# Two layers of a graph network on one core: every sixty-fourth tile of gathered rows fetched by SP, one row per transfer

## The chip, the core and the metric

The kernel runs on one core of a Trainium2 chip. A core has five engines with an instruction queue each: TensorE (PE, with its weight loads shown as PEld), VectorE (DVE), ScalarE (ACT), GpSimd (POOL) and SyncE (SP). SP does no arithmetic on data: it issues transfers and waits. The time is that of one execution on the device in microseconds (us); lower is better.

## What is computed

6250 nodes have 160 features each (64 scalars and 32 vectors of three), and 200,000 edges carry messages from a source node to a destination node. Both layers gather the source node's row for each edge, multiply it with the edge's attributes, and sum the messages by destination. Cut to what matters:

```python
# layer 0: s, v = scalars and vectors of x; src, dst = ends of the edges; e0, e1 from edge_attr_4
ss, vv = (s[src], v[src])
m = concatenate([out0(ss, vv, e0, e1), out1(ss, vv, e0, e1)])
m_agg = segment_sum(m, dst, num_segments=n)
x1 = layernorm(x + x + relu(m_agg @ Ws, m_agg @ Wv))

# layer 1: l = linear(x1) * a;  w = relu(edge_attr_10 @ W_fc1) @ W_fc2
y0, y1 = l0[edge_src], l1[edge_src]
m0, m1, m2, m3 = products of w, y0, y1, e0, e1
s = segment_sum(m, edge_dst, num_segments=N)
out = layernorm(x1 + self_interaction(x1) + 0.5 * linear(s))
```

The edges come sorted by destination; the sources are random, so their rows have to be gathered.

## The kernel before

**Tiles and chunks.** The edges are cut into chunks of 512 (`CH`), 391 of them (`NCH`). A chunk is four tiles (`J`) of 128 edges; partition p of a chunk holds edges 4p to 4p+3, and tile j the j-th of each four. `srcs` holds all source numbers on the chip, 128 partitions x 391 chunks x 4. The gathered rows of a chunk are one buffer `G[c]` of 128 x 4 x 160 floats, from a ring of eight buffers (`GRING`, pool `g`).

**The gather.** `gathered` (L241) issues four indirect transfers from POOL for a chunk, one for each tile: each takes 128 row numbers, one of each partition, and fetches 128 rows of 640 bytes from the table in device memory. The table is `in_x` in layer 0 and `ytab` in layer 1; `ytab` is written by layer 0, block by block. The first three chunks of layer 0 go into a buffer of their own, `early`, which later holds edge attributes.

**Order.** The order of the work on each engine is written out by hand (`manual_schedule`), step by step, in the loop at L615. At step t each stage f with a lag handles the chunk at position t − lag of `ORDER` (a list that mixes chunks of the first part of the edges with chunks of the last part). So an engine's queue holds its share of step t, then its share of step t + 1. The stages of layer 0 are `load` at lag 0, `onehot` 1, `add` 3 and `matmuls` 2; those of layer 1 `load` 0, `joined` 4, `onehot` 1, `hidden` 1, `add` 4, `message` 2 and `matmuls` 3, in this order within a step. In words:

- `load` issues the gathers on POOL (L243). In layer 1 it issues on SP the edge attributes `et` for four chunks at a time (L377), into `w_or_et` and `early` in turn. `attributes` (L403) issues on SP the `raw` attributes of up to 32 chunks in four transfers; `turn` has DVE turn them round.
- `onehot` (L416, L420) has DVE build the selection matrices `S` (a ring of three) from `rel` and the attributes.
- `hidden` (L429, L432) has PE and ACT build `h` from `et`; `message` (L442, L445, L450) has PE multiply `h` with `fc2` and DVE multiply the result with `G[c]`.
- `matmuls` (L462) has PE sum by destination, from `G[c]` in layer 0 and from the messages in layer 1; `joined` (L469, ACT) and `add` (L483 to L487, DVE) add the result to the accumulator `acc` at an address that DVE loads into a register (`low`, L475, eight at a time).

**Blocks.** A block is 128 nodes; there are 49. When its last chunk is done (`CLOSE`), the block's own steps are put into the order, some steps later: in layer 0 SP fetches `xt` (L531), PE projects (L506), ACT rectifies and clears (L542, L543), DVE normalises, and at the end `written` sends `ytab` from ACT (L499) and `btab` from SP (L582). In layer 1 SP fetches `base` (L531) and sends `out` (L499).

**Preparation.** At step 8 of layer 0 (`PREPARE`) `prepare` loads the weights: SP issues some 35 small transfers, PE forms five products (L300), DVE puts them in place (L314 to L349).

**SP's queue.** SP issues nearly all transfers other than the gathers, in the order of the steps. A transfer that has to wait (for a buffer, for data to send) holds all those behind it. Each transfer of SP and ACT uses one of eight completion semaphores in turn, and waits for the transfer that used it before.

Of the kernel before, what the change touches and what calls it, by code (L numbers as in the profile page):

```python
# [10 lines left out]
F32 = mybir.dt.float32  # L11
BF16 = mybir.dt.bfloat16
I32 = mybir.dt.int32
AF = mybir.ActivationFunctionType
# [4 lines left out]
P = 128  # L19
N = 6250  # L20
E = 200000
D = 160
M0, M1 = 64, 32
J = 4
CH = P * J
NCH = -(-E // CH)
# [19 lines left out]

FINAL = NCH - 25
AHEAD = 3
FOLD = 104


# [15 lines left out]
def interleaved():  # L67

    units, groups = HALF // 8, list(range(HALF, NCH, 4))
    order = []
    for u in range(units):
        order += range(8 * u, 8 * u + 8)
        while len(groups) > 3 and (17 - (len(groups) - 3) + 1) * units <= (u + 1) * 18:
            order += range(groups[0], min(groups.pop(0) + 4, NCH))
    for g in groups:
        order += range(g, min(g + 4, NCH))
    return order


ORDER = interleaved()
POS = {c: i for i, c in enumerate(ORDER)}
# [33 lines left out]
def gnn_kernel(ctx: ExitStack, tc: tile.TileContext, x, src, dst, ea, sh, avec,  # L117
# [11 lines left out]
    nc = tc.nc  # L129
    weights = (w1t, w2t, w3t, w4t, w5t, ws, wv, wsi0, wsi1, wl10, wl11, w00, w10, w01, w11, wfc1, wfc2)  # L130
    keep = ctx.enter_context(tc.tile_pool(name="keep", bufs=1))
    rel = keep.tile([P, NCH, J], F32, name="rel")
    srcs = keep.tile([P, NCH, J], I32, name="srcs")
    low = keep.tile([1, NWIN + 1], I32, name="low")
    fits = keep.tile([1, 1], I32, name="fits")
    ident = keep.tile([P, P], F32, name="ident")
    ramp = keep.tile([P, P], F32, name="ramp")
    iota = ramp[:, 0:W]
    early = keep.tile([P, AHEAD, J, D], F32, name="early")
    ahead = {}  # L140
    with tc.manual_schedule(), tc.tile_pool(name="ends", bufs=1) as ep, \
# [8 lines left out]

        first = ep.tile([P, AHEAD, J], I32, name="first")
        nc.sync.dma_start(first, src[:, 0:AHEAD, :])
        nc.scalar.dma_start(dsts, dst)
        nc.sync.dma_start(srcs, src)

        for i in range(AHEAD):
            ahead[i] = gathered(nc, early[:, i], first, x, i)
# [22 lines left out]
        late = NCH - HALF  # L180
        folds = [(k, FOLD, slice(FOLD * k, FOLD * k + FOLD)) for k in range(3)]
        folds += [(3 + h, late, slice(HALF + h, NWIN, 2)) for h in range(2)]
        consts = pp.tile([FOLD, 2, 5], F32, name="consts")
        bounds = ep.tile([FOLD, 2, 5], F32, name="bounds")
        ends = ep.tile([FOLD, 2, 5], F32, name="ends")
        nc.vector.memset(bounds[:, 0, :], 1.0)
# [11 lines left out]
        for a, op in enumerate((ALU.max, ALU.min)):  # L198
            nc.vector.tensor_reduce(mm[:, a, :], rel, AX.X, op)
            tp = pp.tile([FOLD, 4, P], F32, name=f"tp{a}")  # L200
            for k in range(4):
                n = FOLD if k < 3 else late
                nc.tensor.transpose(tp[0:n, k, :], mm[:, a, FOLD * k:FOLD * k + n], ident)
# [22 lines left out]
        for rows, wins, chunks in parts:  # L226
            n = chunks.stop - chunks.start
# [5 lines left out]
    go = nc.values_load(fits[0:1, 0:1], min_val=0, max_val=1,  # L233
                        skip_runtime_bounds_check_because="a comparison's result")
    with tc.If(go > 0) as both:
        windowed(tc, x, srcs, rel, low, ident, iota, early, ahead, ea, sh, avec, *weights, out)
    with both.Else():
        general(tc, x, srcs, rel, dst, ea, sh, avec, *weights, out)


def gathered(nc, g, srcs, table, c):  # L241
    for j in range(J):
        nc.gpsimd.indirect_dma_start(out=g[:, j, :], out_offset=None, in_=table,  # L243
                                     in_offset=bass.IndirectOffsetOnAxis(ap=srcs[:, c, j:j + 1], axis=0))
    return g


@with_exitstack
def windowed(ctx: ExitStack, tc: tile.TileContext, x, srcs, rel, low, ident, iota, early, ahead, ea, sh, avec,
             w1t, w2t, w3t, w4t, w5t, ws, wv, wsi0, wsi1, wl10, wl11,  # L250
             w00, w10, w01, w11, wfc1, wfc2, out):

# [3 lines left out]
    nc = tc.nc  # L256
# [94 lines left out]
    def sums(layer, table, gp, hp):  # L351
        with ExitStack() as s:
            wp = s.enter_context(tc.tile_pool(name=f"w{layer}", bufs=2))
            np_ = s.enter_context(tc.tile_pool(name=f"n{layer}", bufs=2))
            if not layer:
                pn = s.enter_context(tc.tile_pool(name="pn", bufs=1, space=PSUM))
                up = s.enter_context(tc.tile_pool(name="up", bufs=1))
            pa = s.enter_context(tc.tile_pool(name=f"pa{layer}", bufs=3 if layer else 4, space=PSUM))
            if layer:
                ph_ = s.enter_context(tc.tile_pool(name="ph", bufs=1, space=PSUM))  # L360
                pp = s.enter_context(tc.tile_pool(name="pp", bufs=2, space=PSUM))
            s.enter_context(tc.manual_schedule())
            G, S, SH, ET, H, M, PA, AT, RAW = {}, {}, {}, {}, {}, {}, {}, {}, {}

            def load(c):
                if layer or c not in ahead:
                    G[c] = gathered(nc, gp.tile([P, J, D], F32, name="g"), srcs, table, c)
                else:
                    G[c] = ahead.pop(c)
                if c % 4 == 0 and layer:  # L370

                    et = w_or_et if POS[c] % 8 >= 4 else early.rearrange("p a j d -> p (a j d)")
                    et = et[:, :2 * CH].rearrange("p (s e) -> p s e", s=2)
                    ET[c // 4] = et
                    for i in range(2):
                        if c + 4 <= NCH:
                            nc.sync.dma_start(et[64 * i:64 * i + 10, :, :],  # L377
                                              ea[:, c * CH:(c + 4) * CH].rearrange("f (s i e) -> f s i e", s=2, i=2)[:, :, i, :])
                        else:
                            for k in range(c + i, NCH, 2):  # L380
                                nc.sync.dma_start(et[64 * i:64 * i + 10, (k - c) // 2, :], ea[:, k * CH:(k + 1) * CH])
                for first, n in GROUPS:
                    if fetched[first] == POS[c]:
                        attributes(first, n)
# [12 lines left out]
            def attributes(first, n):  # L397

                raw = RAW[first] = hp.tile([P, 512], F32, name="raw")
                if n < 32:  # L400
                    nc.vector.memset(raw, 0.0)
                for q in range(4):
                    nc.sync.dma_start(raw[32 * q:32 * q + n, :],  # L403
                                      sh[first:first + n, 32 * q:32 * q + 32, :].rearrange("c p f -> c (p f)"))
# [115 lines left out]
            def normed(name, b):  # L520
                r = rows(b)
                rs = np_.tile([P, 1], F32, name="rs")
                nc.vector.reciprocal(rs[:r], T.pop(("sd", b))[:r])  # L523
                o = T[name, b] = T.pop(("z", b))
                nc.vector.tensor_scalar(o[:r], o[:r], T.pop(("mv", b))[:r, 0:1], rs[:r],  # L525
                                        op0=ALU.subtract, op1=ALU.mult)
# [77 lines left out]
                sent_rows(nc.sync, b, out[b * P:b * P + rows(b), :], T.pop(("o", b)))  # L604

            if layer:
                stages = [(load, 0), (joined, 4), (onehot, 1), (hidden, 1), (add, 4), (message, 2), (matmuls, 3)]
                parts = [(fetch_base, 3, 2), (project_last, 5, 4), (residual_last, 6, 5), (deviation, 7, 5),
                         (sent, 8, 6)]
            else:  # L610
                stages = [(load, 0), (onehot, 1), (add, 3), (matmuls, 2)]
                parts = [(fetch, 4, 1), (project, 6, 3), (rectify, 6, 4), (residual, 8, 4), (deviation, 9, 4),
                         (lambda b: normed("x1", b), 10, 5), (turned, 11, 5), (kept, 12, 5), (linear, 13, 7),
                         (written, 14, 7)]
# [15 lines left out]
    with tc.tile_pool(name="g", bufs=GRING) as gp, tc.tile_pool(name="sh", bufs=1) as hp:  # L630
        sums(0, x, gp, hp)
        sums(1, ytab, gp, hp)
# [388 lines left out]
```

## Time and profile before

| | us |
|---|---|
| median of three runs | 3960.12 (3959.2 to 3963.18) |
| the profiled execution | 3964.59 |
| its span, first to last instruction | 3962.8 |
| mean granted TensorE clock | 0.78 (0.57 between 100 and 1950 us, 0.99 between 1990 and 3930) |
| gathers from `in_x` in the ring: 1552 | busy 1468.9, mean 0.946 each, idle before them 472.8 |
| gathers from `ytab`: 1564 | busy 1479.2, mean 0.946 each, idle before them 497.7 |

The two layers are about equally long: layer 0 ends near 1960 us, layer 1 begins at 1984. In a list of waits each line has the engine and line that waited, what ended the wait, the total in us, how often, and the longest. "issue" is time in which an engine waited for nothing that the profile shows. In a timeline a line has the start, the duration, engine, line, operation, what is written and read, how many instructions are merged into the line, and in brackets the idle time before it and what ended it. SPq, ACTq and DVEq are the engines' queues: issues of transfers, register loads, waits. An SP line's duration is that of the issue, not of the transfer.

### The profile page before, as it was taken

How to read it: one execution, taken by the hardware profiler on the slowest of the kernel's cores; microseconds unless marked ns; L12 is line 12 of the kernel's file. 1: busy time of each engine (PE TensorE's matmuls, PEld its weight loads, DVE VectorE, ACT ScalarE, POOL GpSimd, SP SyncE). 2: the span in 40 equal slices, each digit the busy share in tenths (PEclk: the TensorE clock that was granted, in tenths of full speed). 3: DMA queues.
4: the chain of work that ended last, by engine and by line, in shares of the span. 5: the costliest groups of instructions: out<-in, count | busy, mean ns of one | idle time of the engine just before them, and what ended most of it. 6: DMA issues, size and time to landing. Idle time of an engine off the chain costs nothing. (4 is left out here: it accounts for less than half of the span.)

```text
span 3962.8 us, 42550 instructions
## 1 busy us (share of the span) xinstructions
PE 3250.1 (82%) x12754; PEld 2152.7 (54%) x12755; DVE 2032.2 (51%) x6485; ACT 478.4 (12%) x1217; POOL 2960.1 (75%) x3133
## 2 busy tenths in 40 slices
PE   4777777777777777777788898998999999999998
PEld 3444444444444445455555566665666666666665
DVE  4223222233333333344456666666666677777776
ACT  2000000000000000001111111111111111111111
POOL 7777777777777777777677777777777777777775
PEclk7555555565565656566699999999999999999999
DMA  3222222223232323233222222222333333232332
GB/s 86 74 66 66 71 74 69 74 71 79 71 77 74 76 72 78 75 79 81 71 72 73 71 76 73 75 74 74 75 80 76 78 76 77 74 81 75 80 77 66
DMA packets 198440, 295.63 MB, mean 75 GB/s; under 512 B 59462, under 2 KB 140860, under 8 KB 198202
## 3 DMA queue, kind: packets, MB, share of 16 engines
q0 software_dynamic: 150144, 256.45, 26.3%
q1 hardware_dynamic: 40870, 31.56, 2.7%
q10 hardware_dynamic: 7188, 4.80, 0.4%
q8 instruction: 107, 1.75, 0.2%
q14 instruction: 131, 1.07, 0.1%
HBM read 280.57 MB, written 12.00 MB: 74 GB/s over the span
## 5 line engine op out<-in xcount | busy, mean ns | idle before, releaser
L243 POOL DMA_INDIRECT g<-ytab,srcs x1564 | 1479.2, 946 | 497.7 <-issue 394.5
L243 POOL DMA_INDIRECT g<-in_x,srcs x1552 | 1468.9, 946 | 472.8 <-issue 396.3
L462 PE MATMUL ab<-g,S 128*128 128x160 f32 (+1 forms) x3736 | 1177.5, 494 | 502.4 <-DMA g<-in_x,srcs 380.6
L462 PEld LDWEIGHTS ab<-g,S 128*128 128x128 f32 (+1 forms) x3736 | 724.5, 287 | 964.9 <-DMA g<-in_x,srcs 669.5
L462 PE MATMUL ab<-m,S 128*128 128x320 f32 (+1 forms) x3760 | 958.3, 446 | 6.8 <-DVE acc L487 6.3
L442 PE MATMUL pw<-fc,h 100*128 100x192 f32 x3128 | 663.5, 343 | 158.2 <-DVE m L450 73.8
L442 PEld LDWEIGHTS pw<-fc,h 100*128 100x128 f32 x3128 | 503.8, 191 | 426.1 <-issue 301.5
L462 PEld LDWEIGHTS ab<-m,S 128*128 128x128 f32 (+1 forms) x3760 | 612.5, 193 | 220.7 <-issue 40.7
L485 DVE STREAM_TRANSPOSE ab<-ab 128x160 f32<-128x160 f32 x470 | 170.5, 363 | 946.1 <-PE ab L462 944.0
L445 DVE TENSOR_TENSOR m<-pw,g 128x256 f32<-128x256 f32 x782 | 330.3, 422 | 520.8 <-DMA g<-ytab,srcs 439.1
L450 DVE TENSOR_TENSOR m<-g,pw 128x192 f32<-128x192 f32 x1564 | 475.9, 346 | 0.0
L420 DVE TENSOR_TENSOR S<-bank,sh 128x384 f32<-128x384 f32 (+2 forms) x782 | 431.5, 552 | 65.9 <-PE ab L462 15.8
L487 DVE TENSOR_TENSOR acc<-acc,ab 128x120 f32 (+2 forms) x940 | 261.4, 278 | 212.8 <-ACT acc L543 140.2
L469 ACT ACTIVATE ab<-ab 32x160 f32<-32x160 f32 x470 | 121.2, 265 | 1350.8 <-PE ab L462 1151.9
L432 ACT ACTIVATE h<-ph 100x512 f32<-100x512 f32 x391 | 228.5, 585 | 207.4 <-PE ph L429 203.6
L416 DVE TENSOR_TENSOR bank<-ramp,rel 128x96 f32<-128x96 f32 (+2 forms) x782 | 199.4, 255 | 21.3 <-PE bank L593 21.0
L483 DVE STREAM_TRANSPOSE ab<-ab 128x160 f32<-128x160 f32 x470 | 167.4, 356 | 13.1 <-issue 8.5
L506 PE MATMUL ph<-w_or_et,acc 128*128 128x160 f32 (+1 forms) x490 | 138.1, 466 | 1.7 <-DVE acc L487 1.3
L506 PEld LDWEIGHTS ph<-w_or_et,acc 128*128 128x128 f32 (+1 forms) x490 | 129.2, 328 | 11.9 <-issue 8.8
L542 ACT ACTIVATE rl<-ph 128x160 f32<-128x160 f32 (+1 forms) x49 | 14.9, 303 | 931.2 <-PE ph L506 930.6
L429 PE MATMUL ph<-early,fc 10*100 10x512 f32 x392 | 112.5, 637 | 2.4 <-DMA early<-in_ea 2.4
L429 PE MATMUL ph<-w_or_et,fc 10*100 10x512 f32 x390 | 109.8, 632 | 1.8 <-DMA w_or_et<-in_ea 1.8
(94 smaller groups left out, 820.0 us busy)
## 6 DMA issues: line engine op xcount, KB each, us to landing
g<-ytab,srcs POOLq DMA_INDIRECT x1564
g<-in_x,srcs POOLq DMA_INDIRECT x1552
raw<-in_sh SPq DMA_DIRECT2D x88, 64.0 KB
early<-in_ea SPq DMA_DIRECT2D x98, 40.0 KB
xt<-in_x SPq DMA_DIRECT2D x48, 80.0 KB
ytab<-y ACTq DMA_DIRECT2D x48, 80.0 KB
btab<-base SPq DMA_DIRECT2D x48, 80.0 KB
w_or_et<-in_ea SPq DMA_DIRECT2D x96, 40.0 KB
```

What stands on the lines that cost most here:

```text
L243: nc.gpsimd.indirect_dma_start(out=g[:, j, :], out_offset=None, in_=table, in_offset=bass.IndirectOffsetOnAxis(ap=srcs[:, c, j:j + 1], axi ...
L416: nc.vector.tensor_tensor(oh[:, :, :w], iota[:, None, :w].to_broadcast([P, J, w]), rel[:, c, :, None].to_broadcast([P, J, w]), op=ALU.is_e ...
L420: nc.vector.tensor_tensor(S[c][:, :, :, :w], oh[:, :, None, :w].to_broadcast([P, J, 4, w]), attr[:, :, :, None].to_broadcast([P, J, 4, w]) ...
L429: nc.tensor.matmul(ph[:, i, :], fc1[g:g + 10, :], ET[c // 4][g:g + 10, c % 4 // 2, :], start=True, stop=True)
L432: nc.scalar.activation(H[c], H["p"][:, c % 2, :].rearrange("f (p j) -> f j p", j=J), AF.Relu, scale=FC_SCALE)
L442: nc.tensor.matmul(pw[:, j, :], h[:, q + j, :], fc2, start=True, stop=True)
L445: nc.vector.tensor_tensor(mq[:, :, :, 0:64], pw[:, :, 0:128].rearrange("p j (a u) -> p j a u", a=2), y[:, :, None, 0:64].to_broadcast([P, ...
L450: nc.vector.tensor_tensor(mq[:, :, a, 64:160].rearrange("p j (d u) -> p j d u", d=3), y1, pw[:, :, None, w:w + 32].to_broadcast([P, 2, 3, ...
L462: nc.tensor.matmul(ab[:, :n], one[h * i:h * i + h, j, :, :], t[h * i:h * i + h, j, :], start=(j == 0), stop=(j == J - 1), skip_group_check ...
L485: nc.vector.transpose(tr, blocks[:, 0])
L487: nc.vector.tensor_tensor(v, v, tr[:, :, :width(c)], op=ALU.add)
L506: nc.tensor.matmul(po[:r], lhs, weights[:, g, :], start=(g == 0), stop=(g == 4))
```

## The change

At positions 15, 31, 47, ... 383 of both layers, 24 in each, POOL issues three gathers for the chunk, and not four. The rows of the chunk's last tile come by SP. They are spread over the sixteen steps up to the chunk's own `load`: at each step SP loads eight row numbers of the tile into eight registers (one instruction), and then issues eight transfers of one row of 640 bytes, from an address made of the register, to one partition of a buffer `row` (two of these). The program has one instruction of register arithmetic ahead of each such transfer. The numbers of a tile are fetched as one line of 128 from `in_src` to a single partition (`num`), half a period ahead. At the step after the chunk's `load`, ACT copies the buffer `row` into the last tile of `G[c]`; the copy is the first thing in ACT's queue of that step, and waits for the rows and for the chunk's three gathers. In SP's queue the rows of a step stand ahead of everything else of the step.

All else is as before: the rings, the lags, the arithmetic. SP's program grows from 681 transfers to 6873 (with the general path, which isn't taken), with 6144 instructions of register arithmetic and 768 loads of eight registers; POOL's has 48 gathers fewer, ACT's 48 copies more.

```diff
+EVERY = 16
+ROWS = P // EVERY
...
-def gathered(nc, g, srcs, table, c):
-    for j in range(J):
+def gathered(nc, g, srcs, table, c, tiles=J):
+    for j in range(tiles):
         nc.gpsimd.indirect_dma_start(out=g[:, j, :], out_offset=None, in_=table,
                                      in_offset=bass.IndirectOffsetOnAxis(ap=srcs[:, c, j:j + 1], axis=0))
...
+            rp = s.enter_context(tc.tile_pool(name=f"r{layer}", bufs=2))
...
+            helpers = {EVERY - 1: (nc.sync, mybir.EngineType.SP)}
+            helped = {ORDER[i] for i in range(EVERY // 2, NCH) if i % EVERY in helpers}
+
+            def numbers(c):
+                NUM[c] = rp.tile([1, P], I32, name=f"num{POS[c] % EVERY}")
+                nc.sync.dma_start(NUM[c], src[:, c, J - 1:J].rearrange("p a -> a p"))
+
+            def fetch_rows(c):
+                i = POS[c]
+                for place, (queue, engine) in helpers.items():
+
+                    k = (i - place - 1) % EVERY
+                    due = i - k + EVERY - 1
+                    if due >= NCH or ORDER[due] not in helped:
+                        continue
+                    d = ORDER[due]
+                    if d not in NUM:
+                        numbers(d)
+                    if d not in ROW:
+                        ROW[d] = rp.tile([P, D], F32, name=f"row{place}")
+                    if k == EVERY // 2 and due + EVERY < NCH:
+                        numbers(ORDER[due + EVERY])
+                    a = k * ROWS
+                    _, at = nc.values_load_multi_w_load_instructions(
+                        NUM[d][0:1, a:a + ROWS], engines=[engine], min_val=0, max_val=N - 1,
+                        skip_runtime_bounds_check_because="node numbers")
+                    for n in range(ROWS):
+                        queue.dma_start(ROW[d][a + n:a + n + 1, :], table[ds(at[n], 1), :])
+
+            def place_rows(c):
+                if c in helped:
+                    del NUM[c]
+                    nc.scalar.activation(G[c][:, J - 1, :], ROW.pop(c), AF.Copy)
+
             def load(c):
                 if layer or c not in ahead:
-                    G[c] = gathered(nc, gp.tile([P, J, D], F32, name="g"), srcs, table, c)
+                    G[c] = gathered(nc, gp.tile([P, J, D], F32, name="g"), srcs, table, c, J - (c in helped))
...
-                stages = [(load, 0), (joined, 4), (onehot, 1), (hidden, 1), (add, 4), (message, 2), (matmuls, 3)]
+                stages = [(fetch_rows, 0), (load, 0), (place_rows, 1), (joined, 4), (onehot, 1), (hidden, 1), (add, 4), (message, 2), (matmuls, 3)]
...
-                stages = [(load, 0), (onehot, 1), (add, 3), (matmuls, 2)]
+                stages = [(fetch_rows, 0), (load, 0), (place_rows, 1), (onehot, 1), (add, 3), (matmuls, 2)]
```

In the changed program `fetch_rows` issues the numbers at L375, loads the registers at L393 and issues the rows at L397; the copy of `place_rows` is L402, and the gathers are L246.

More of the change, by code (lines that the diff above doesn't have):

```diff
@@ L235, in gnn_kernel @@
     with tc.If(go > 0) as both:
-        windowed(tc, x, srcs, rel, low, ident, iota, early, ahead, ea, sh, avec, *weights, out)
+        windowed(tc, x, srcs, src, rel, low, ident, iota, early, ahead, ea, sh, avec, *weights, out)
     with both.Else():
         general(tc, x, srcs, rel, dst, ea, sh, avec, *weights, out)
-def gathered(nc, g, srcs, table, c):
-    for j in range(J):
+def gathered(nc, g, srcs, table, c, tiles=J):
+    for j in range(tiles):
         nc.gpsimd.indirect_dma_start(out=g[:, j, :], out_offset=None, in_=table,
@@ L248, in windowed @@
 @with_exitstack
-def windowed(ctx: ExitStack, tc: tile.TileContext, x, srcs, rel, low, ident, iota, early, ahead, ea, sh, avec,
+def windowed(ctx: ExitStack, tc: tile.TileContext, x, srcs, src, rel, low, ident, iota, early, ahead, ea, sh, avec,
              w1t, w2t, w3t, w4t, w5t, ws, wv, wsi0, wsi1, wl10, wl11,
@@ L362, in sums @@
             s.enter_context(tc.manual_schedule())
-            G, S, SH, ET, H, M, PA, AT, RAW = {}, {}, {}, {}, {}, {}, {}, {}, {}
+            G, S, SH, ET, H, M, PA, AT, RAW, NUM, ROW = ({} for _ in range(11))
+            helpers = {EVERY - 1: (nc.sync, mybir.EngineType.SP)}
[27 more added lines that the diff above has]
+                    nc.scalar.activation(G[c][:, J - 1, :], ROW.pop(c), AF.Copy)
             def load(c):
                 if layer or c not in ahead:
-                    G[c] = gathered(nc, gp.tile([P, J, D], F32, name="g"), srcs, table, c)
+                    G[c] = gathered(nc, gp.tile([P, J, D], F32, name="g"), srcs, table, c, J - (c in helped))
                 else:
```

## The prediction

> **What bounds the kernel now.** I read the page's busy times first, then the waits of POOL, then POOL's timeline, then who waits for the gathers, and last the rows of SP.
>
> ```profile
> span 3962.8 us, 42550 instructions
> PE 3250.1 (82%) x12754; PEld 2152.7 (54%) x12755; DVE 2032.2 (51%) x6485; ACT 478.4 (12%) x1217; POOL 2960.1 (75%) x3133
> ...
> POOL 7777777777777777777677777777777777777775
> ```
>
> PE is the busiest, yet POOL is the engine whose digit never changes. Its waits (total us, times, longest) say why:
>
> ```profile
> POOL g L243 <- issue: 790.8, 2596, 0.3
> POOL g L243 <- PE ab L462: 60.9, 200, 0.3
> ...
> POOL g L243 <- DMA ytab<-y: 21.6, 1, 21.6
> ```
>
> Every idle stretch is 0.3 us, whatever is named as its end, except one of 21.6 us between the layers. So POOL's 25% of idle time is the fixed gap between two gathers, and not waiting. Its timeline at the layer boundary shows the beat (start, duration, and the idle time before in brackets):
>
> ```profile
> 1959.14 0.95 POOL L243 DMA_INDIRECT g<-in_x,srcs  x1 [0.30 <-issue]
> 1960.39 0.95 POOL L243 DMA_INDIRECT g<-in_x,srcs  x1 [0.30 <-issue]
> 1961.64 0.94 POOL L243 DMA_INDIRECT g<-in_x,srcs  x1 [0.30 <-issue]
> 1984.20 0.94 POOL L243 DMA_INDIRECT g<-ytab,srcs  x1 [21.62 <-DMA ytab<-y]
> ```
>
> The first layer's 1552 ring gathers start at 21.21 us and the last at 1961.64: 1940.43 / 1551 = 1.251 us each. The second layer's 1564 run from 1984.20 to 3938.61: 1954.41 / 1563 = 1.250. A chunk of four gathers takes 5.00 us, and 391 chunks twice are almost the whole span. The consumers wait for it:
>
> ```profile
> PEld ab L462 <- DMA g<-in_x,srcs: 669.5, 894, 2.2
> DVE m L445 <- DMA g<-ytab,srcs: 439.1, 400, 2.5
> ```
>
> In layer 1 the slack of the next engine is small: between 1990 and 3930 us PE is busy 1778.41 us of 1940, that is 4.58 us of a 5.00 us chunk.
>
> **What the change takes away.** At positions 15, 31, ... 383 (24 in each layer) POOL issues three gathers for the chunk, not four: 48 × 1.25 = 60.0 us off the beat that sets the span. A period of 16 chunks takes 63 × 1.25 = 78.8 us, or 4.92 us a chunk. PE's 4.58 still fits, and DVE's wait of 439.1 / 391 = 1.1 us a chunk is more than the 0.08 asked of it.
>
> **What it adds on SP.** At every one of the 384 steps of a layer up to position 383 SP loads eight node numbers into registers, then issues eight transfers of one row, each with an instruction of register arithmetic ahead of it. The trace has no transfer with an address from a register, so I bound a row from the nearest lines (min/median/max ns):
>
> ```profile
> L582 SPq DMA_DIRECT2D btab<-base x49: 246/327/352, 401.9 to 1981.1; - x49
> L377 SPq DMA_DIRECT2D early<-in_ea x98: 282/300/1455, 30.7 to 3889.7; - x98
> L475 DVEq TENSOR_LOAD <-low x118: 593/596/1149, 28.0 to 3937.2; - x118
> L487 DVEq FUSED_REGOPS  x940: 69/69/69, 29.2 to 3949.9; - x188
> 68.39 0.42 SPq L340 DMA_DIRECT2D wc<-in_w  x1
> 68.86 0.89 SPq L342 DMA_DIRECT2D wc<-in_w  x2
> 69.79 0.42 SPq L343 DMA_DIRECT2D wc<-in_w  x1
> ```
>
> Issue: 0.246 us is the shortest (the last block, 106 rows), 0.282 the shortest of 20 runs of 2 KB, 0.42 that of a back-to-back burst of 32 rows, whose pitch (68.39 to 69.79, three transfers) is 0.465, hence 0.045 between instructions. I take 0.30, near the low end, since one row is the smallest transfer, with 0.05 for the unseen address. Register arithmetic: DVE's 0.069. A row is 0.069 + 0.045 + 0.30 + 0.045 = 0.46 us; with the ends 0.246 and 0.42 it is 0.405 and 0.58. The load of eight registers is 0.596 + 0.045 = 0.64, from DVE's row. A step: 8 × 0.46 + 0.64 = 4.32 (3.88 to 5.28).
>
> SP's older work by step: layer 0 per 16 chunks two blocks (0.40 + 0.33 + gaps, 1.6 us), two raw transfers (0.9), one of node numbers (0.5): 3.0 / 16 = 0.19. Layer 1 has eight et transfers of 0.35 as well, with base and out of two blocks: 6.2 / 16 = 0.39. So SP needs 4.51 us a chunk in layer 0 and 4.71 in layer 1 against POOL's 4.92. It keeps up as long as a row costs below (4.92 − 0.64 − 0.19) / 8 = 0.51 us, or 0.49 in layer 1. That is the whole question.
>
> Completion: in the built program each SP transfer waits for the one eight before it. In the burst above the 14 transfers of wc keep 0.465 without a stall, so each landed within 8 × 0.465 = 3.7 us; eight rows take 3.68. No added wait, if rows land no slower.
>
> The Trainium skill speaks against the change: "DMA: Bandwidth & Descriptors", section "Rules for kernel authors", tells to coalesce many small transfers, and its section "Anatomy of one DMA — SWDGE (gpsimd) path" gives about 2.0 us fixed for one. By it, as an estimate, 128 rows one after the other would take 256 us. The burst's row, 0.465 apart, shows that they overlap, and decides. The same page's section "Issuing engines are not separate DMA queues" holds that issuing elsewhere only saves sequencer time, usually small; here POOL's beat is such time, and it is the span.
>
> **What is queued behind SP's new work.** The first raw transfers (18.90 us) move behind two number loads, their landing, a register load and eight rows: 0.93 + 1.0 + 0.64 + 3.68, to 25.1. The weights of `prepare` stand behind nine steps, 8 × 4.32 after raw: they begin near 62 and, at their present durations (5.4 and 11.4 us), end near 78.6 in place of 73.0. DVE waits for wc till 74.50 now, and PE goes on with chunk 8 at 76.72, so that chunk is done at 82.3 + 1.5 = 83.8. POOL needs its ring slot for chunk 16 at 81.2 + 3.75 = 85.0: covered by 1 us. Row 15's last part then lands near 78.6 + 7 × 4.32 + 2 = 111, chunk 15 is done near 113, and POOL needs its slot at 85 + 35 = 120. Covered by 7 us; later SP gains (4.92 − 4.51) × 16 = 6.6 us a period. At 0.51 us a row both covers are gone.
>
> Later SP is held at a block's store (L582, L499) until the computation reaches the same step, about three chunks behind POOL. A row issued then is needed after about two more chunks, 10 us, against 4.3 to issue and 2 to land: covered. At the layer boundary SP begins layer 1's rows with POOL at 1984 and ends the first tile after 16 × 4.71 = 75 us, POOL's chunk 15 after 79.
>
> **On ACT**: 48 copies of 128x160, about 0.3 us each by L542's 303 ns, ACT busy 12%. The copy stands at step 16k, ahead of `joined` and `hidden`, and waits for the chunk's three gathers too. That holds layer 1's chain some 4 us once in 16 chunks, made good at 4.92 − 4.58 = 0.34 a chunk; the eight slots cover 39 us. Only after position 383 is there no time left to make it good: +1 us at the end.
>
> **Sum.** Against the profiled run's own 3964.6 us (span 3962.8 and 1.8 around it): −60.0 + 1 = 3905.6. The median of the three runs, 3960.1, is 4.5 below the profiled one, so the forecast is 3901, with 3897 to 3915 for this case (nothing lost, or 14 us lost at the start).
>
> **Rivals.** *SP becomes the bound* (slower). Place: L397 in the new program. For it: the burst's 0.42 is as much a row as 0.30 is, and it gives 0.58 a row. Against it: the shorter issues of the smaller transfers. It decides from 0.50 us a row; beyond it each 0.01 costs 768 × 8 × 0.01 = 61 us. At 0.52: about 3900 + 122 = 4020. At 0.58: 384 × (5.47 + 5.67) = 4278, plus the 120 us of start, boundary and ends: about 4400.
>
> *Half of it*: layer 1 stays at 5.00 us, since SP needs just 0.2 us less than POOL there, or PE and the waiting copy eat the slack: 3960 − 30 + 1 = 3931. For it: PE's 92% there. Against it: DVE's 1.1 us of waiting.
>
> *Nothing*: rows land so late that the ring fills each period and gives back what was won: 3960. For it: only SP's narrow margin; the eight slots speak against it.
>
> **Chances.** Forecast case 0.60, half 0.06, no change 0.04, SP the bound 0.30. A change under 0.2% can't be told from none here, so faster 0.66, same 0.04, slower 0.30. Within the slow case half lies beyond 0.535 us a row, 4110 us, so the range goes from 3896 to 4100 and leaves some 0.15 above and 0.04 below.
>
> **What would show it.** Right: SP's row issues at L397 pitched 0.40 to 0.50 us; POOL's timeline still at 1.25 us with no waits above 0.3 but at the boundary; 3068 gathers. Wrong: a pitch above 0.51, POOL waiting for ACT or PE once a period, or ACT's L402 waiting long for the row transfers while SP has no wait of its own. If POOL's beat between gathers itself lengthens, the sum's first term is wrong.

## The result, and the profile after

| | kernel before | kernel after |
|---|---|---|
| median, us | 3960.12 (3958.48 to 3963.18, 5 runs) | 3992.21 (3985.14 to 4001.66, 5 runs) |
| the profiled execution | 3964.59 | 3998.08 |
| its span | 3962.8 | 3996.3 |

The ratio is 1.0079, with a 95% interval of 1.0068 to 1.009: slower by 0.8%, where 1.5% faster was forecast. The time lies in the stated range (3896 to 4100), on the wrong side of the kernel before.

First the page of the kernel after, the lines that answer to those shown of before:

```profile
span 3996.3 us, 62132 instructions
...
PE 2984.6 (75%) x12754; PEld 2126.7 (53%) x12755; DVE 2004.4 (50%) x6485; ACT 486.5 (12%) x1265; POOL 2917.6 (73%) x3085
...
POOL 7777777777777777777477777777777777667663
```

POOL's digit is now 4 in one slice in the middle, and falls towards the end. The list of waits of the same kernel (total us, times, longest) says what is new:

```profile
POOL g L246 <- issue: 822.2, 2687, 3.0
ACT g L402 <- DMA row<-in_x: 722.0, 23, 71.9
...
DVE z L587 <- DMA xt<-in_x: 290.3, 27, 21.6
...
PE ph L468 <- DMA early<-in_ea: 75.9, 26, 8.8
...
POOL g L246 <- DVE m L489: 40.8, 65, 4.8
...
POOL g L246 <- DMA row<-ytab: 37.5, 1, 37.5
```

Three kinds of transfer that are SP's come late: `xt` (a block's rows of layer 0; before, the list had no such wait), `et` (into `early` and `w_or_et`; before, PE waited 2.4 and 1.8 us for it in all, now 75.9 and 53.9), and the new rows. The ring's gathers on POOL now wait up to 4.8 us for DVE, where before none of their waits but the one at the boundary passed 0.3. POOL's timeline at that boundary:

```profile
1934.12 0.94 POOL L246 DMA_INDIRECT g<-in_x,srcs  x1 [0.30 <-issue]
1972.55 0.94 POOL L246 DMA_INDIRECT g<-ytab,srcs  x1 [37.49 <-DMA row<-ytab]
```

From the first and last gathers in such timelines the span falls into four parts. The last column is the kernel with the two edits found below; the shortfall is the kernel after minus that one (each figure is rounded by itself).

| us of the profiled span | before | after | both edits | shortfall of after |
|---|---|---|---|---|
| to the end of layer 0's last gather | 1962.6 | 1935.1 | 1934.3 | 0.7 |
| wait at the boundary | 21.6 | 37.5 | 15.2 | 22.3 |
| layer 1, first to last gather | 1955.4 | 1975.0 | 1927.0 | 48.0 |
| from there to the end | 23.2 | 48.8 | 17.7 | 31.1 |
| sum | 3962.8 | 3996.3 | 3894.2 | 102.1 |

Layer 0 gains POOL 27.5 us of the 30 forecast. All that is lost is lost at the boundary, in the second half of layer 1 and after the last gather.

**The price of a row was not the cause.** The rows of SP by line (ns: min/median/max), of the kernel after:

```profile
L397 SPq FUSED_REGOPS  x6144: 37/37/51, 21.8 to 3935.9; - x199
L397 SPq MOVE row<-in_x x3072: 29/29/38, 21.9 to 1926.5; - x192
L397 SPq DMA_DIRECT2D row<-in_x x3072: 224/228/322, 22.0 to 1926.6; - x192
```

```profile
L393 SPq TENSOR_LOAD <-num x768: 550/782/983, 21.2 to 3932.2; - x192
```

A row is one instruction of register arithmetic, a move and the issue, with short gaps: 0.411 us from one to the next (median), below the 0.46 that was taken and the 0.51 at which SP would have become the bound. A step by these is 8 × 0.411 + 0.78 = 4.07, and a tenth of all steps, from the start of one to the start of the next, are done in 4.13 us or less. Yet SP took (1926.6 − 22.0) / 384 = 4.96 us a step in layer 0 and (3936.0 − 1971.7) / 384 = 5.12 in layer 1, where POOL's own pace is 4.92. The rest is SP's older transfers and waiting.

**Layer 0: SP waits for ACT, several steps ahead.** The largest but one of SP's own waits, of the same kernel:

```profile
SPq L397 <- DMA ytab<-y: 163.4, 31, 18.8
```

31 times a row transfer waits for `ytab`, 163.4 us in all. A row of `in_x` has no need of `ytab`; what they share is the eight completion semaphores. One of these waits is 16.6 us long and ends at 502.02. ACT's timeline there, with the transfer that ends it:

```profile
499.88 0.39 ACT L616 ACTIVATE y<-pl,a_sb 128x160 f32<-128x160 f32 x1 [11.46 <-PE pl L610]
500.31 0.34 ACTq L538 DMA_DIRECT2D ytab<-y  x1
```

The order in the program as built shows how the two are tied. These are SP's transfers with the number of the semaphore that each waits for and takes over, read from the list of its instructions, with the steps counted by the register loads (the transfers in the trace have the same turns):

```
step 97  row  semaphores 3 4 - 6 7 0 1 2 3      5 is left out: ACT's ytab has it
step 98  row  semaphores 4 5 6 7 0 1 2 3        the second row waits for that ytab
...
step 101 row  semaphores 5 6 7 0 1 2 3 4
step 101 btab semaphore 5                       btab of the same block
```

The block's `ytab` belongs to step 101: the `btab` that the code issues right after it is SP's last transfer of step 101. But its turn among the eight came in SP's step 97. The semaphores were not dealt in the order of the steps; ACT's transfer was put 4 steps early here, and 7 for the next block (taken in step 103, `btab` in step 110). So SP, at step 98, waits until the computation has done step 101. It can't be ahead; it is pinned behind. By the timelines SP loads the numbers of step 104 at 527.4 us, 15.8 us after DVE built that step's selection matrix, and those of step 184 at 941.7, 36.5 us after. (With the two edits of the next section these are 510.2 and 902.7 us, 1.2 and 0.1 before DVE's.) Everything else that SP sends stands in that queue, `xt` too, fetched only four steps ahead of its use. The ring of eight hides it from POOL, so layer 0 loses nothing until its end, where the last blocks' `ytab` come late: 37.5 us.

**Layer 1: a loop through SP.** A stretch of the chain of work that ended last (start, us, what), of the kernel after:

```profile
3462.29 0.97 SPq L393
...
3466.39 0.23 SPq L397
...
3466.71 1.90 DMA early<-in_ea
...
3468.75 1.60 PE ph L468 x4
3470.36 2.86 PE pw L481 x8
3473.22 3.94 PE ab L501 x8
...
3484.43 0.36 DVE z L564
3484.79 0.22 DVE bank L455
3485.01 0.19 SPq L538
...
3485.24 0.93 SPq L393
```

Read it as a circle. SP loads eight numbers and issues eight rows (4.4 us); only then `et` (1.90 us), which PE needs one step later (`hidden`, L468); PE and DVE work; DVE finishes a block; SP's store of that block (L538) has waited for it; and behind the store stand the next rows and the next `et`. One turn here is 22.95 us for four steps, 5.7 us a step against POOL's 4.92. PE waited for `et` before 3300 us too, 76 of the 130 us in all, and POOL kept its beat; why the circle closes only there isn't shown. Once it is closed it is the pace: from 3312 us on POOL took 79.0 to 90.5 us for 63 gathers (16 chunks), and not 78.8.

### The profile page after: what moved, and what is told of

It is laid out like the page before. It is cut to its first block, busy times and chain, and to the rows that moved or that the text cites. A ratio compares the mean times of both kernels' runs of the same rounds, so it can differ in the third digit from the quotient of the medians.

```text
span 3996.3 us, 62132 instructions
## 1 busy us (share of the span) xinstructions
PE 2984.6 (75%) x12754; PEld 2126.7 (53%) x12755; DVE 2004.4 (50%) x6485; ACT 486.5 (12%) x1265; POOL 2917.6 (73%) x3085
## 4 chain that ended last, share of the span: by engine, by line
PE 34%; SPq 23%; issue 16%; POOL 11%; DMA 10%; DVE 5%; ACT 1%; DVEq 0%; ACTq 0%; POOLq 0%
PE ab L501 17%; SPq L397 16%; POOL g L246 11%; PE pw L481 9%; SPq L393 5%; PE ph L468 4%; DMA g<-in_x,srcs 4%; DMA g<-ytab,srcs 2%; DVE m L489 1%; PE bank L632 1%; DMA early<-in_ea 1%; DMA w_or_et<-in_ea 1%; PE ph L545 1%; PE pl L610 1%; DVE m L484 1%
## 5 line engine op out<-in xcount | busy, mean ns | idle before, releaser
L246 POOL DMA_INDIRECT g<-ytab,srcs x1540 | 1458.1, 947 | 554.4 <-issue 405.3
L246 POOL DMA_INDIRECT g<-in_x,srcs x1528 | 1447.1, 947 | 466.4 <-issue 416.9
L501 PE MATMUL ab<-g,S 128*128 128x160 f32 (+1 forms) x3736 | 904.2, 432 | 738.3 <-ACT g L402 315.9
L501 PEld LDWEIGHTS ab<-g,S 128*128 128x128 f32 (+1 forms) x3736 | 649.0, 264 | 996.1 <-DMA g<-in_x,srcs 340.0
L501 PE MATMUL ab<-m,S 128*128 128x320 f32 (+1 forms) x3760 | 986.7, 459 | 2.3 <-DVE acc L526 2.1
L501 PEld LDWEIGHTS ab<-m,S 128*128 128x128 f32 (+1 forms) x3760 | 635.9, 202 | 227.5 <-issue 61.9
L481 PEld LDWEIGHTS pw<-fc,h 100*128 100x128 f32 x3128 | 551.5, 203 | 243.5 <-issue 153.1
L524 DVE STREAM_TRANSPOSE ab<-ab 128x160 f32<-128x160 f32 x470 | 168.7, 359 | 564.5 <-PE ab L501 560.4
L468 PE MATMUL ph<-early,fc 10*100 10x512 f32 x392 | 131.8, 680 | 76.2 <-DMA early<-in_ea 75.9
L468 PE MATMUL ph<-w_or_et,fc 10*100 10x512 f32 x390 | 126.6, 658 | 54.4 <-DMA w_or_et<-in_ea 53.9
L545 PE MATMUL ph<-w_or_et,acc 128*128 128x160 f32 (+1 forms) x490 | 113.7, 401 | 40.6 <-DVE acc L526 40.1
L545 PEld LDWEIGHTS ph<-w_or_et,acc 128*128 128x128 f32 (+1 forms) x490 | 103.5, 270 | 51.4 <-issue 42.5
```

The lines of the kernel that those rows point to most:

```text
L468: nc.tensor.matmul(ph[:, i, :], fc1[g:g + 10, :], ET[c // 4][g:g + 10, c % 4 // 2, :], start=True, stop=True)
L481: nc.tensor.matmul(pw[:, j, :], h[:, q + j, :], fc2, start=True, stop=True)
L501: nc.tensor.matmul(ab[:, :n], one[h * i:h * i + h, j, :, :], t[h * i:h * i + h, j, :], start=(j == 0), stop=(j == J - 1), skip_group_check ...
L545: nc.tensor.matmul(po[:r], lhs, weights[:, g, :], start=(g == 0), stop=(g == 4))
```

## The experiments

Two edits undo one of these each, and leave rows, register loads and copies as they are. The first, in `written`:

```diff
-                sent_rows(nc.scalar, b, ytab[b * P:b * P + r, :], y)
+                sent_rows(nc.sync, b, ytab[b * P:b * P + r, :], y)
```

The second takes the `et` part out of `load` into a stage of its own, three steps earlier:

```diff
+            def edges(c):
+                if c % 4 == 0:
...
-                stages = [(fetch_rows, 0), (load, 0), (place_rows, 1), (joined, 4), (onehot, 1), (hidden, 1), (add, 4), (message, 2), (matmuls, 3)]
+                stages = [(edges, -3), (fetch_rows, 0), (load, 0), (place_rows, 1), (joined, 4), (onehot, 1), (hidden, 1), (add, 4), (message, 2), (matmuls, 3)]
...
+            if layer:
+                for i in range(3):
+                    edges(ORDER[i])
```

The first edit changes two things at once, the engine that sends `ytab` and the place of its turn among the semaphores.

A third kernel gives the rows four steps more of lead, to test the rival that rows late at ACT's copy are all there is to it (at the price of two tiles, 46 and not 48):

```diff
-            helped = {ORDER[i] for i in range(EVERY // 2, NCH) if i % EVERY in helpers}
+            helped = {ORDER[i] for i in range(EVERY, NCH) if i % EVERY in helpers}
...
-                i = POS[c]
+                i = POS[c] + 4
                 for place, (queue, engine) in helpers.items():
```

**The first four runs.** ytab by SP:

> The changed kernel, with one edit: in layer 0 ytab is sent by SP, right before btab, and no longer by ACT. Theory (completion semaphores): SP and ACT share eight of them, dealt in turn when the program is built; there the ytab transfer of a block stands up to 7 steps before SP's rows of the same step, so a row at SP's step 97 waits for ytab of step 101, and SP runs 14 to 37 us behind DVE in layer 0. With ytab in SP's own order this wait (163 us in 31 waits at L397) goes, SP runs level with DVE or ahead, DVE's wait for xt (290 us) goes, and the wait of POOL at the boundary falls from 37.5 to about 22 us: 3992 - 16 = 3976; layer 1 as it is. Rival (SP's work): SP is late because rows take too long to issue; 49 more transfers of 0.35 us make it later: 3992 to 4000, xt as late as before. Rival (rows late at ACT's copy alone): as the first, no change, 3992.

et earlier:

> The changed kernel, with one edit in layer 1: the edge attributes et of a group of four chunks are issued by SP three steps before the step in which they stand now, where they come behind the eight rows of their step and are needed one step later. Theory (a loop through SP): in the second half of layer 1 et lands late, PE's hidden layer waits, DVE then ends the block late, SP's out store waits for DVE, and the next rows and et stand behind that store. With et three steps (12 to 15 us) earlier the loop opens: PE's waits for et (130 us in all) go, the beat of POOL holds, layer 1's gathers take 1925 and not 1975 us, and the tail after the last gather is about 24 and not 49 us: 3992 - 50 - 25 = 3918; up to 3945 if the rows, still one step ahead of their use, hold ACT. Rival (SP's work): SP issues as much as now, so it stays as late: 3992. Rival (rows late at ACT's copy): 3985 to 3992.

Both:

> The changed kernel with both edits, ytab sent by SP in layer 0 and et three steps earlier in layer 1. Theory (semaphores and loop): the gains add, 3918 - 16 = 3902, close to 60 us below the kernel before; up to 3930 if rows still hold ACT. Rival (SP's work): 3992 or more. Rival (rows late at ACT's copy): 3985 to 3992.

Rows with more lead:

> The changed kernel with one edit: the sixteen steps over which a tile's rows are issued end four steps earlier (five steps of lead at ACT's copy, not one); the tile at position 15 is gathered by POOL in both layers, so 46 gathers fewer, not 48 (+2.5 us). SP's work, ytab and et stay. Theory (semaphores and loop): ACT's copy no longer waits for rows in layer 1, but et still lands late and SP is still held by ytab: 3980 to 4000. Rival (rows late at ACT's copy are what holds the chain): the copies' waits and the lateness both go: 3905 to 3930. Rival (SP's work): 3992, rows later again by as much as SP falls behind.

None came out as any theory had it. On this chip the kernel before itself took 4829.63 us, and the four took 5843.61, 5884.34, 5883.23 and 5714.75. SP was slow in a way that the first profile doesn't have, so the kernel after was run beside the edits once more:

> The changed kernel itself, beside the next three on one chip. The four runs so far were on a chip where the kernel before took 4830 us, not 3960, and where SP, in stretches, started its instructions only 0.70 or 1.40 us apart (some 1600 such intervals; none in the changed kernel's first profile); they say nothing on the two theories. On a chip where the kernel before takes 3960: 3992. On one where it takes 4830: about 5880, like the four kernels that differ little from it.

> The edit of e1_ytab_sp again (ytab sent by SP, in SP's own order). On a chip where the kernel before takes 3960: theory (completion semaphores) 3976, POOL's wait at the boundary 22 and not 37 us, DVE's wait for xt gone; rival (SP's work) 3992 to 4000 with xt as late as before.

> The edit of e2_et_early again (et three steps earlier in layer 1). On a chip where the kernel before takes 3960: theory (loop through SP) 3918, up to 3945 if the rows hold ACT; layer 1's gathers take 1925 and not 1975 us. Rival (SP's work) 3992.

> The edits of e3_both again (both). On a chip where the kernel before takes 3960: theory 3902, up to 3930 if the rows hold ACT; rival (SP's work) 3992 or more.

That was another such chip: before 4866.12, after 5948.73, ytab by SP 5945.53, et earlier 5977.19, both 5982.9. SP's row transfers, of the kernel after on that chip:

```profile
L397 SPq DMA_DIRECT2D row<-in_x x3072: 1/228/1406, 22.6 to 3001.2; - x192
```

The median is that of the first chip, 228 ns, but single ones last 1.4 us: in stretches SP starts an instruction every 0.70 or 1.40 us, whatever it is. The mean pitch of rows within a step is 0.79 us (0.45 on the first chip), and a step takes 7.59 us on average (5.10). SP waited 313 of the 5914 us of the profiled span there, against 492 of 3996 on the first chip. That speaks for SP's issuing as the bound there, but it isn't shown; PE and POOL, too, were held for hundreds of us by causes that this profile doesn't name. The edits did not help: on the second such chip they moved the time by −3 to +34 us. More lead for the rows (5714.75, ratio 1.1828 against 1.2107 for ytab by SP on that chip) helped some. Why the kernel before takes 22% more there too isn't known, since no profile of it was had on such a chip. The run meant for that met a chip like the first:

> The kernel before itself, for its profile on the chip at hand. On the two chips of the first eight runs it took 4830 and 4866 us, not 3960, and the changed kernel 5949. If the chip is like the first one: 3960, POOL's beat 1.25 us throughout. If it is like those two, two theories: (a) every gather takes longer or is further apart, a beat near 1.53 us throughout; (b) the beat is 1.25 us wherever POOL can go on, and there are holes in which engines wait for nothing that the profile shows (PE's weight loads on 'issue', as for 1015 us in the changed kernel there), because instructions reach the engines late. In (b) a program with 20,000 instructions on SP in place of 900 is hit the hardest on SP.

It took 3960.11 us, which leaves both theories on the slow chips untried. Eight more runs of the same edits followed. Three fell on a slow chip at once:

> The edit of e1_ytab_sp (ytab sent by SP, in SP's own order), meant for a chip where the kernel before takes 3960, as it did in the last run. Theory (completion semaphores): 3976, POOL's wait at the boundary 22 and not 37 us, SP's 163 us of waiting for ytab and DVE's 290 us of waiting for xt gone. Rival (SP's work): 3992 to 4000 with xt as late as before.

> The edit of e2_et_early (et three steps earlier in layer 1), for a chip where the kernel before takes 3960. Theory (loop through SP): 3918, up to 3945 if the rows hold ACT; layer 1's gathers take 1925 and not 1975 us. Rival (SP's work): 3992.

> The edits of e3_both (both), for a chip where the kernel before takes 3960. Theory: 3902, up to 3930 if the rows hold ACT; rival (SP's work): 3992 or more.

5950.63, 5985.04 and 5995.69 us, before 4872.0. And two later, meant to divide the gain between the edits:

> The edit of layer 0 alone (ytab sent by SP), on a chip where the kernel before takes 3960. If the two edits act each in its own layer: POOL's wait at the boundary is 15 us as with both edits, layer 0's gathers end at 1934, and layer 1 is as in the changed kernel (gathers 1975 us, tail 49 us), so the span is 1949 + 1975 + 49 = 3973 and the time 3975. If the lateness of layer 1 is carried over from layer 0: near 3895 to 3920. On a chip like the slow ones 5950.

> The edit of layer 1 alone (et three steps earlier), on a chip where the kernel before takes 3960. If the two edits act each in its own layer: layer 0 and the boundary as in the changed kernel (layer 1 begins at 1972.6), and layer 1 as with both edits (gathers 1927 us, tail 18 us): 1972.6 + 1927 + 17.7 = 3917, time 3919. If layer 1 needs both: above 3950. On a chip like the slow ones 5980.

5852.89 and 5886.97 us, before 4823.59: no more is learnt from these five than from the first. What follows is from the three that met chips on which the kernel before takes 3960 to 3962.

**Both edits.**

> The two edits of e3_both in one kernel: ytab sent by SP (layer 0), et three steps earlier (layer 1). On a chip where the kernel before takes 3960: theory (semaphores in layer 0, a loop through SP in layer 1) 3902, up to 3930 if the rows hold ACT. In layer 0 SP's waits for ytab and DVE's for xt go and POOL waits 22 and not 37 us at the boundary; in layer 1 the gathers take 1925 and not 1975 us and the tail is 24 and not 49 us. Rival (SP's work): 3992 or more, layer 0's xt as late as before, layer 1's gathers 1975 us. On a chip like the slow ones: 5950 to 6000, and the question stays open.

3895.26 us (3893.95 to 3896.72), ratio 0.9835 (0.9819 to 0.9851): faster than the kernel before by 1.6% and than the kernel after by 97 us. The theory's 3902 is met within 7 us; the boundary and the end came out 7 and 6 us better than it had them. SP's issue work, the rival, is out: SP issues the same rows at the same 228 ns, and 50 transfers more. Its list of waits for POOL, which answers to the first one:

```profile
POOL g L246 <- issue: 771.7, 2532, 0.3
...
POOL g L246 <- DMA row<-ytab: 15.2, 1, 15.2
```

No wait of the ring's gathers but the boundary's passes 0.3 us, apart from one for PE of 1.1. DVE's wait for `xt` and PE's for `et` are gone from the list. SP still waits, for the data that it has to send:

```profile
SPq L540 <- ACT y L618: 151.6, 34, 11.4
SPq L540 <- DVE bank L457: 93.6, 36, 11.2
```

These waits don't show in POOL's beat. SP is level with DVE: it loads the numbers of step 336 at 3598.3 us, DVE builds that step's matrix at 3598.4. In layer 1 the rows of every tile are issued 5.6 to 18.7 us before the chunk's own gathers are done.

**Each alone.** Layer 0's edit:

> The edit of layer 0 alone (ytab sent by SP), on a chip where the kernel before takes 3960. Each edit acting in its own layer: boundary wait 15 us, layer 1 as in the changed kernel (gathers 1975 us, tail 49 us): 3975. If layer 1's lateness is carried over from layer 0: 3895 to 3920. On a chip like the slow ones 5950.

3973.23 us (3966.2 to 3979.41), ratio 1.0034 (1.0022 to 1.0045). Its waits:

```profile
PE ph L468 <- DMA early<-in_ea: 74.6, 27, 8.0
...
POOL g L246 <- DMA row<-ytab: 15.6, 1, 15.6
```

The boundary is 15.6 us, SP's waits at the rows for `ytab` are gone from its list, though SP now has `ytab` itself to send, and layer 1 is as slow as in the kernel after (1972.0 us of gathers, 48.9 after them): each edit acts in its own layer. Layer 1's edit:

> The edit of layer 1 alone (et three steps earlier), on a chip where the kernel before takes 3960. Each edit acting in its own layer: layer 1 begins at 1973 as in the changed kernel and takes 1927 us of gathers and 18 us of tail as with both: 3919. If layer 1 needs both edits: above 3950. On a chip like the slow ones 5980.

3917.51 us (3914.1 to 3918.25), ratio 0.9891 (0.9875 to 0.9908). Its waits:

```profile
DVE z L589 <- DMA xt<-in_x: 288.8, 27, 21.6
...
POOL g L246 <- DMA ytab<-y: 35.7, 1, 35.7
```

The reverse: `xt` and the boundary as late as in the kernel after, layer 1 as fast as with both (1925.6 and 17.6 us). The single gains, 19 and 75 us, add to 94 of the 97.

**Rows with more lead, once more.**

> The edit of e4_rows_lead (rows end four steps earlier, 46 tiles and not 48), on a chip where the kernel before takes 3960. Theory (semaphores and loop): et still lands late in layer 1 and SP is still held by ytab in layer 0: 3980 to 4000, with PE's waits for et near the 130 us of the changed kernel. Rival (rows late at ACT's copy): 3905 to 3930. On a chip like the slow ones 5715.

5708.67 us beside 4830.03 for the kernel before: a slow chip. Whether more lead for the rows alone would have done on a chip like the first stays open; that it isn't needed is shown, since with both edits the rows have the lead that the change gave them. The traces speak against this rival for layer 1. ACT's waits there for the rows, of the kernel after and then of both edits:

```profile
ACT g L402 <- DMA row<-ytab: 37.9, 12, 5.6
```

```profile
ACT g L402 <- DMA row<-ytab: 97.6, 20, 7.0
```

ACT waits more for rows in the kernel that is 97 us faster, and in neither does PE wait for a copy in layer 1. In layer 0 of the kernel after PE did wait for the copies, 316 us in 21 waits (37 in 3 with both edits), but POOL's gathers there ended only 0.7 us later than with both edits.

## Why the prediction was wrong

- **The beat, −60.0 us: right.** POOL stays at 1.25 us a gather wherever it isn't held. With both edits 57 of the 60 appear (28.3 and 28.4 us in the two layers), and 6.4 at the boundary and 5.5 after the last gather, which the sum didn't have. That their 3895 us is so near the forecast of 3901 is in part luck.
- **The price of a row, 0.46 us within 0.405 to 0.58: right, on the dear side.** 0.411 on chips like the first. The load of eight registers was taken as 0.64 and is 0.78. The step of 4.32 is 4.13 where SP does nothing else and waits for nothing. The rival "SP becomes the bound" was held to decide from 0.50 us a row; it didn't decide here. The chance of 0.30 on slower had the sign, with the wrong mechanism, and that 3992 lies in the range is luck: the range reached to 4100 for a dear row, and the row was cheap. On the slow chips, at 0.79 us, it may be what happens.
- **Completion, "No added wait, if rows land no slower": this step failed.** The eight semaphores were checked against SP's rows alone. ACT takes from the same eight, and its turns were dealt up to seven steps ahead of SP's. Measured: 163.4 us in 31 waits at the rows, and 22 us of the span, at the boundary; the edit that takes `ytab` off ACT gave 19 us.
- **What is queued behind the rows: this step failed for `et`.** The prediction followed a row behind a store ("needed after about two more chunks, 10 us … covered"), and with both edits rows behind a store are covered. It counted the `et` transfers in SP's load, 0.35 us each, but not that they stand behind the eight rows of their step and are needed one step later. Measured: 130 us of PE waiting, 54 of it after 3300 us, and 48 + 31 us of the span, in the second half of layer 1 and after its last gather; the edit of `et` alone gave 75 us.
- **The start: right.** Row 15's last part was put near 111 us and was issued at 109.0; POOL's slot came at 121.4 (120).
- **The boundary: "SP begins layer 1's rows with POOL at 1984" missed what delays `ytab` itself.** By the prediction's own sum, 30 us saved in layer 0 and the wait as before, POOL would begin layer 1 near 1954. It began at 1972.6, and with both edits at 1949.6.
- **The copies: right.** With both edits the +1 us at the end that the sum had for them can't be seen.
- **Half, and nothing, as rivals:** PE's 4.58 us a chunk was no limit; with both edits layer 1 keeps POOL's 4.92. In the kernel after PE itself was slower as well. Windows of it from 3300 us on (busy us of PE, PEld, DVE, ACT, POOL; granted clock, DMA share, GB/s), and then of both edits:

```profile
3300.00:3900.00 600.00, 549.14 (x2375) 396.04 (x2376) 405.39 (x1267) 101.11 (x272) 420.41 (x444) 0.91 0.29 73
```

```profile
3300.00:3800.00 500.00, 470.04 (x2177) 321.97 (x2176) 371.35 (x1152) 94.32 (x249) 378.44 (x400) 1.00 0.29 79
```

The granted clock was 0.91 where PE waited for `et`, and 1.00 where it didn't; with the edit of `et` alone it was 0.99, with that of `ytab` alone 0.91. A matmul took 549.14 / 2375 = 0.231 us there against 470.04 / 2177 = 0.216, 7% more. As an estimate from these, PE's 4.58 us a chunk became 4.9: the slack against POOL's 4.92, by which the prediction wanted to make good what the copies hold, was gone as long as PE waited for `et`. So part of the 79 us may be the slower PE and not the waiting itself; no run divides the two. The Trainium skill, "TensorE: Matmul & The Clock Gate", section "Part 1: The HAM clock gate", says that the clock falls after an idle window of some 3.4 us; the waits for `et` in that stretch, of up to 5.1 us, and the two clocks agree with it. The rule that spoke against the change, to coalesce small transfers (the same skill, "DMA: Bandwidth & Descriptors", section "Rules for kernel authors"), wasn't what decided: 128 rows a tile, 0.411 us apart, kept up on such chips wherever the order let them.

## What to carry to other kernels

A queue with room to spare in us per step can still be late: ask of each thing in it what it waits for, and at which step of the computation that is done. Transfers of two engines that share completion semaphores are tied to each other in the order in which these were dealt, which may not be the order of the steps; look for the number that is missing from one queue's turn. Before putting work at the head of a queue, list what then stands behind it and how many steps ahead of its use that is; give the shortest of these its lead first.

## What the runs showed of the hardware

- The same program can take 22% longer: the kernel before took 3960 to 3962 us in some runs and 4824 to 4872 in others. In the latter a program with 20,000 instructions on SP lost 18 to 23% against the kernel before; SP's instructions came 0.70 and 1.40 us apart in stretches, and DVE stood still, for up to 14.8 us, on what the profile calls "remote" (655 us in 85 waits at L524). What is behind it wasn't found. That it is a matter of the chip, as "slow chip" has it above, isn't shown either: on record the runs of layer 0's edit alone (before: 3961.74) and of the rows with more lead (before: 4830.03) have the same chip number, seven minutes apart.
- The issue of a row with a register address took 228 ns, less than the shortest issue with a fixed address before the change (246 ns, 106 rows); with its register arithmetic (37) and its move (29) it is 294 ns. No run has a single row with a fixed address to compare.
